# Groups of small products in seven forms among the warm-up products of a planned one-core kernel

## The chip, the cores and the metric

The kernel runs on one core of a Trainium2 chip. The metric is the device time of one execution in microseconds (us). The engines of a core work through queues of their own, in order: TensorE (PE, matrix products into PSUM; PEld is its weight load), VectorE (DVE), ScalarE (ACT), GpSimd (POOL), and SyncE (SP), which issues the DMAs.

## What is computed

The input x has 8 sequences of 512 rows and 128 columns, in fp32. Four blocks follow each other, each with a layernorm ahead and a residual: a scan (a gated state space model, "mamba"), a mixture of eight experts, a windowed attention with 16 heads, and the same mixture of experts again.

```
x = x + scan(layernorm(x))
x = x + experts(layernorm(x))
x = x + attention(layernorm(x))
x = x + experts(layernorm(x))

scan:      h = x W_in; xb, zb = halves of h, each: convolution over 3 steps, silu
           delta = softplus(dt W_dt + b_dt), clipped; b, c = tanh(...)
           decay = exp(-delta a), clipped;  state = decay * state + (1 - decay) * b * xb
           y = sum(state * c) + D * xb;     out = [y, zb] W_out
experts:   cw = softmax(x w_router) * softmax(10 x w_gating), normalised over the 8 experts
           out = sum over e of cw[e] * (silu(x w_gate[e]) * (x w_up[e])) w_down[e]
attention: softmax(q k + mask) v, chunks of 10 rows with 25 rows of left context
```

## The kernel before

Fp32 accuracy of the large products is reached with pairs: each operand is split into a rounded part and the rest (fp32r "hi" and "lo"), and one product becomes three (`matmul3`). An expert's work on one sequence is cut into four quarters of its 512 inner columns. A quarter has three products g (gate), three u (up) and three y (down). Between them ACT, DVE and POOL make h: silu of g, times u, the hi part, the lo part. For the first sequence the first four experts work on half a sequence (256 rows) at a time, the rest on 512.

The order of the instructions is written by a planner while the program is built. Each piece of work is a generator (a "lane") that yields the engine it needs next; `Clock` keeps an estimated end for every engine, and `Lanes.tick` (line 314) takes the lane that can start soonest. The estimated times only set the order: on the chip each engine runs its queue in order and waits on semaphores. All instructions pass through the wrapper `Engine`, so nearly every line of the profile names line 254 (`f(*args, **kw)`); groups are told apart by tile names.

Names that matter here. `x_m`, `tp_m`, `mxt`, `mh`, `mv`, `mxb`, `mzb`, `mde`, `mbc`: the scan block up to its rows. `mbx`: b spread over the state, then times xb; `mdec`: the decays, clipped on DVE by `cap`; `mst`: the scans; `mcc`, `mcx`: c times state; `macc`: their sum; `mo`: the output product. `tp_f`, `xt_f`, `lps`, `rps`, `pr`, `cw`, `cps`: layernorm, routing and weights of the experts; `cwb` is the weight of one expert spread over the partitions by a DMA, `y` times `cwb` is added up in `acc`, and `yp` transposes it back. `as`, `aw`, `ao`, `amt`: attention products in bf16 or with 32-column outputs. `wg`, `wu`, `wd` are the expert weights, loaded and split during the first 100 us.

The scan of the first sequence runs alone at the start, in two halves (`first_halves`, line 668), since the experts can't begin without it. The scan of sequence 1 runs beside the experts of sequence 0, and so on. ACT loads a function table whenever the next function isn't in the loaded one (line 533 and, without a call of `table`, line 254); `hidden` (line 1158) uses tanh and two DVE instructions instead of silu while the table with exp and tanh is loaded and the planner's clock is before `clock.hold`.

While the planner waits for the first expert inputs, the loop at line 1619 ticks the lanes; when none can start, it issues one dummy product into the bank `warm`, of the constant `sel` with itself (128x128 times 128x256, fp32r), and moves the planner's TensorE clock on by 0.1. Nothing reads `warm`. PSUM has eight banks; up to `AT_FIRST` = 7 of them may be held by work other than experts until the experts begin (`sides`, line 399), `warm` among them.

## Time and profile before

| | us |
|---|---|
| median of 3 runs | 1391.99 |
| lowest and highest of them | 1391.98, 1397.03 |
| the profiled execution, its own time | 1392.73 |
| its span, first to last instruction | 1390.9 |
| TensorE busy | 1353.4 (97%) |
| VectorE, ScalarE, GpSimd busy | 1053.2, 963.0, 944.5 |
| mean granted TensorE clock | 0.988 of full |

The profiled execution is one execution with the hardware profiler on. Its span runs from the first to the last instruction, and its own time holds some work around that. Rows of the order of time give start, duration, engine, line, operation, output tile, input tiles and shape; "[idle before <- X]" is the time that the engine waited and what ended it. Products on TensorE overlap, so the distance from start to start tells what one costs, not its duration.

### The profile page before, as it was taken

What the parts mean: (1) busy time and instruction counts of PE and PEld (TensorE: products, weight loads), DVE (VectorE), ACT (ScalarE), POOL (GpSimd) and SP (SyncE); (2) the same over time, 40 slices, a digit from 0 to 9 for tenths busy, and PEclk for the clock granted to TensorE, in tenths of its full rate; (3) what the DMA queues carried; (4) which work ended last, traced back from release to release, by engine and by line L of the source; (5) the groups of instructions that cost most, each with busy time, mean ns of one, the idle gap of its engine ahead of it and who ended that gap; (6) DMA issues with size and microseconds to landing.
All of it is one profiled execution on the core that took longest, in us unless ns stands there. A gap on an engine that the chain in (4) does not pass through costs nothing. (4 is left out here: it accounts for less than half of the span.)

```text
span 1390.9 us, 25797 instructions
## 1 busy us (share of the span) xinstructions
PE 1353.4 (97%) x8410; PEld 1085.0 (78%) x8410; DVE 1053.2 (76%) x3090; ACT 963.0 (69%) x1671; POOL 944.5 (68%) x1057
## 2 busy tenths in 40 slices
PE   7779999999999999999999999999999999999998
PEld 6677777777778878788788787787887877787886
DVE  6787888888986457888888888888888888754443
ACT  6568768677765557667777677777777776765654
POOL 4667576576674777666767667676666676777776
PEclk9989999999999999999999999999999999999999
DMA  3221214233126223356545455455564545222211
GB/s 123 73 82 35 69 39 125 59 81 91 35 54 81 55 52 65 84 110 125 129 88 125 100 117 137 78 128 115 105 141 78 116 64 100 53 66 53 39 39 38
DMA packets 256631, 116.28 MB, mean 84 GB/s; under 512 B 107996, under 2 KB 252401, under 8 KB 256497
## 3 DMA queue, kind: packets, MB, share of 16 engines
q1 hardware_dynamic: 256497, 114.64, 38.1%
q8 instruction: 66, 1.08, 0.3%
q14 instruction: 68, 0.56, 0.1%
HBM read 82.22 MB, written 31.98 MB: 82 GB/s over the span
## 5 line engine op out<-in xcount | busy, mean ns | idle before, releaser
L254 POOL TENSOR_TENSOR h<-h,h 128x512 fp32r<-128x512 f32 (+1 forms) x510 | 642.1, 1267 | 278.6 <-ACT h L254 242.5
L254 PE MATMUL u<-xt_f,wu 128*128 128x512 f32 (+1 forms) x1584 | 458.7, 398 | 10.3 <-ACT h L254 4.5
L254 PE MATMUL g<-xt_f,wg 128*128 128x512 f32 (+1 forms) x1584 | 454.4, 395 | 4.1 <-DVE mst L254 3.3
L254 PE MATMUL y<-h,wd 128*128 128x512 f32 (+1 forms) x1584 | 450.5, 394 | 1.9 <-POOL h L254 1.9
L254 ACT CAST h<-h 128x512 fp32r<-128x512 f32 (+1 forms) x476 | 286.4, 605 | 224.6 <-DVE h L254 222.3
L254 DVE TENSOR_TENSOR h<-u,h 128x512 f32<-128x512 f32 (+1 forms) x438 | 292.5, 673 | 180.3 <-PE u L254 126.0
L254 ACT ACTIVATE h<-g 128x512 f32<-128x512 f32 (+1 forms) x528 | 305.1, 583 | 116.2 <-PE g L254 90.2
L254 PEld LDWEIGHTS y<-h,wd 128*128 128x128 f32 x1584 | 290.9, 190 | 70.8 <-POOL h L254 3.0
L254 PEld LDWEIGHTS g<-xt_f,wg 128*128 128x128 f32 x1584 | 288.6, 190 | 70.2 <-DVE mst L254 4.0
L254 PEld LDWEIGHTS u<-xt_f,wu 128*128 128x128 f32 x1584 | 284.7, 189 | 74.9 <-ACT h L254 8.0
L254 POOL TENSOR_TENSOR acc<-acc,cwb 128x512 f32<-128x512 f32 (+1 forms) x115 | 146.9, 1278 | 54.9 <-DVE cwb L254 28.3
L254 DVE CUSTOM_DVE_ANT_0 amasked<-as,maskt 100x125 f32<-100x125 f32 (+2 forms) x640 | 141.6, 278 | 11.4 <-PE as L254 10.9
L254 ACT ACT_TABLE_LOAD x102 | 130.9, 1283 | 16.3 <-PE g L254 14.9
L254 DVE TENSOR_TENSOR apt<-aw,maskk 125x400 f32<-125x400 f32 (+2 forms) x160 | 89.7, 574 | 12.5 <-PE aw L254 12.4
L254 DVE TENSOR_TENSOR cwb<-y,cwb 128x512 f32<-128x512 f32 (+1 forms) x115 | 77.3, 672 | 16.6 <-PE y L254 9.6
L254 ACT ACTIVATE apt<-apt 125x400 f32<-125x400 f32 (+2 forms) x160 | 80.8, 540 | 0.4
L254 DVE SCALAR_TENSOR_TENSOR h<-h,g 128x512 f32<-128x512 f32 (+1 forms) x90 | 58.4, 651 | 18.4 <-ACT h L254 18.2
L254 DVE SCALAR_TENSOR_TENSOR h<-u,h 128x512 f32<-128x512 f32 (+1 forms) x90 | 58.8, 655 | 3.8
L254 PEld LDWEIGHTS <-ks 68*125 68x125 bf16 (+2 forms) x640 | 47.2, 136 | 11.4 <-issue 2.1
L254 PEld LDWEIGHTS <-qs 65*100 65x100 bf16 (+2 forms) x640 | 45.4, 125 | 11.0 <-issue 0.5
L254 DVE DVE_READ_ACCUMULATOR2_ANT amx<- 100x1 f32 (+2 forms) x640 | 51.5, 80 | 0.0
L254 PE MATMUL aw<-qs,ks 68*125 68x100 bf16 (+2 forms) x640 | 49.2, 220 | 0.5 <-DMA qs<-amts 0.5
(195 smaller groups left out, 1241.6 us busy)
## 6 DMA issues: line engine op xcount, KB each, us to landing
cwb<-cwd_f SPq DMA_DIRECT2D x124, 256.0 KB
aqd<-apc SPq DMA_DIRECT2D x64, 192.0 KB
ks<-aqd SPq DMA_DIRECT2D x48, 125.0 KB
qs<-aqd SPq DMA_DIRECT2D x48, 100.0 KB
x_fo<-x SPq DMA_DIRECT2D x16, 256.0 KB
aqd<-apc SPq DMA_DIRECT2D x32, 128.0 KB
x_f<-x SPq DMA_DIRECT2D x15, 256.0 KB
aod<-aos SPq DMA_DIRECT2D x24, 100.0 KB
```

Of the source, the lines that this page charges most:

```text
L254: f(*args, **kw)
```

## The change

`small` is a bf16 copy of the identity, made by one POOL instruction, in a buffer of the pool that later holds `cwb`. A second dummy bank, `warm2`, is taken beside `warm`, and `AT_FIRST` goes from 7 to 8, so that other work may hold as many banks as before. The waiting loop is as it was, but after the planner's time 8.0, and at most fourteen times, a group of small products comes ahead of the dummy: seven forms, each twice in turn. The forms differ in type (bf16 `small` or fp32 `ident`), in the rows of the array (68, 51, 48, 64 or 55, from row 0 or from row 64), in the columns of the output (125, two places of 50, four places of 30 or 32, all 128), in the order in which rows and banks alternate, and in their number (16, 32 or 4). Each product moves the planner's TensorE clock by 0.06 beyond its estimated cost. Nothing reads what they write.

```diff
-AT_FIRST = 7
+AT_FIRST = 8
 WARM = 3.5
+FORMS = 8.0
...
         warm = now(side([P, L], "warm"))
+        warm2 = now(side([P, L], "warm2"))
+        banks = warm, warm2
+        small = fp.tile([P, L], F32, tag="cwb", name="small", bufs=2).bitcast(BF16)[:, :P]
+        pool.tensor_copy(small, ident)
+        tried = []
+
+        def rows(n, t, k, into, form):
+
+            for i in range(n):
+                r = 64 * t(i)
+                form(i, slice(r, r + k), into(i))
+            clock.end["T"] += n * 0.06
+            return clock.end["T"]
+
+        def plain(i, r, o):
+            pe.matmul(o[:125, :100], small[r, :125], small[r, :100], start=True, stop=True)
+
+        def squares(i, r, o):
+            c = i % 2 * 64
+            pe.matmul(o[c : c + 50, :75], small[r, c : c + 50], small[r, :75], start=True, stop=True)
+
+        def strips(i, r, o):
+            c = i % 4 * 32
+            pe.matmul(o[c : c + 30, :55], small[r, c : c + 30], small[r, :55], start=True, stop=True)
+
+        def wide(i, r, o):
+            pe.matmul(o[:, :P], ident[r], ident[r], start=True, stop=True)
+
+        def thin(i, r, o):
+            c = i % 4 * 32
+            pe.matmul(o[c : c + 32, :30], ident[r, c : c + 32], ident[r, :30], start=True, stop=True)
+
+        forms = [
+            lambda: rows(16, lambda i: 0, 68, lambda i: banks[i % 2], plain),
+            lambda: rows(16, lambda i: i % 2, 51, lambda i: banks[i % 2], plain),
+            lambda: rows(16, lambda i: i // 2 % 2, 51, lambda i: banks[i // 2 % 2], plain),
+            lambda: rows(16, lambda i: i // 2 % 2, 48, lambda i: banks[i // 2 % 2], squares),
+            lambda: rows(32, lambda i: i // 4 % 2, 48, lambda i: banks[i // 4 % 2], strips),
+            lambda: rows(4, lambda i: i % 2, 64, lambda i: banks[i % 2], wide),
+            lambda: rows(16, lambda i: i // 4 % 2, 55, lambda i: banks[i // 4 % 2], thin),
+        ]
         while (0, 0) not in ready or ready[0, 0][1] == 0:
             if lanes.tick():
                 continue
             if clock.now > WARM:
                 sel = mc["sel"]
+                if clock.now > FORMS and len(tried) < 2 * len(forms):
+
+                    tried.append(forms[len(tried) % len(forms)])
+                    e = tried[-1]()
                 e = pe.matmul(warm[:, :HALF], sel[:, 0], sel[:, : HALF // P], start=True, stop=True)
                 clock.end["T"] += 0.1
             else:
                 clock.now += 0.03
+        freed(e)
         freed(e)
```

## The prediction

> **What bounds the kernel now.** I read the page's busy times first, then one row per stage, then who TensorE waited for, then the order of time in the stage that the change touches.

> ```profile
> PE 1353.4 (97%) x8410; PEld 1085.0 (78%) x8410; DVE 1053.2 (76%) x3090; ACT 963.0 (69%) x1671; POOL 944.5 (68%) x1057
> ```

> TensorE is busy for 1353.4 of 1390.9 us. The stage rows (length, busy time and instructions of PE, PEld, DVE, ACT, POOL, then granted clock, DMA share, GB/s) say where the other 37.5 us lie.

> ```profile
> 0.00:50.00 50.00, 38.29 (x224) 32.24 (x225) 35.29 (x86) 26.65 (x59) 23.20 (x36) 0.86 0.33 102
> 50.00:100.00 50.00, 38.34 (x237) 32.63 (x236) 39.60 (x94) 33.79 (x79) 35.46 (x49) 0.86 0.29 83
> 110.00:150.00 40.00, 37.84 (x177) 29.09 (x176) 30.96 (x63) 31.90 (x55) 27.14 (x32) 0.96 0.17 40
> 150.00:507.00 357.00, 353.47 (x1655) 278.76 (x1654) 281.65 (x522) 248.75 (x415) 236.62 (x234) 1.00 0.31 69
> 507.00:1380.00 873.00, 871.40 (x6033) 700.04 (x6032) 657.24 (x2305) 613.70 (x1047) 610.07 (x695) 1.00 0.44 91
> ```

> 23.4 us of TensorE's idle time lie in the first 100 us, at a clock of 0.86 instead of 1.00; 2.2 us between 110 and 150, 3.5 us between 150 and 507, 1.6 us from there to 1380, 7.0 us in the tail. The first 100 us are set by other engines, all the rest by TensorE. Who it waited for up to 96 us:

> ```profile
> PE u L254 <- DVE mst L254: 4.3, 1, 4.3
> PE tp_f L254 <- DVE xn_f L254: 3.8, 4, 1.8
> PE mbc L254 <- ACT mxb L254: 3.1, 1, 3.1
> PE g L254 <- DVE mst L254: 2.7, 1, 2.7
> ```

> These are the serial first sequence (mbc, tp_f) and, at 74 to 90 us, VectorE's scans (mst) of the second sequence, behind which the experts' gates queue on VectorE.

> **The change, part by part.** In the built instruction order of the changed kernel only twelve of the fourteen groups appear: the loop ends first, so wide and thin are there once. They hold 212 products; 27 of the 108 old dummies stay, 81 go.

> *Price of the products.* TensorE's order of time (start, duration, operation):

> ```profile
> 607.51 0.89 PE L254 MATMUL ao<-apt,v 125*32 125x100 f32 x32
> 608.33 0.96 PE L254 MATMUL y<-h,wd 128*128 128x512 f32 x3
> 609.13 0.21 PE L254 MATMUL amt<-eye,mp 110*80 110x110 bf16 x1
> 609.16 0.95 PE L254 MATMUL g<-xt_f,wg 128*128 128x512 f32 x3
> 609.94 0.62 PE L254 MATMUL aw<-qs,ks 68*127 68x102 bf16 x8
> 610.38 0.95 PE L254 MATMUL u<-xt_f,wu 128*128 128x512 f32 x3
> ```

> From start to start 8 aw take 0.44 us, 0.055 each; 32 ao take 0.82 us, 0.026 each. So 96 plain products cost 96 x 0.055 = 5.3 us and 32 squares 1.8. The 64 strips cost 1.7 at ao's row, 3.5 at aw's; I take 1.7, the row with the same 32-column outputs. For the fp32 ones the nearest rows are two mde of 64x256 at 65.28 to 65.92 us, 0.32 each, so half, 0.16, for 128 columns: 4 wide cost 0.6; and four lps of 128 columns at 66.97 to 67.53, 0.14 each: 16 thin cost 2.2 at most, 0.5 if their 30 columns count in proportion; I take 1.1. Together 10.5 us (9.7 to 13.4). A change of form costs about 0.09: the u after aw takes 0.79 to the next start (610.38 to 611.17), undisturbed ones 0.70. Twelve groups have 24 changes, 2.2 us. Removed are 81 x 0.126 (9 dummies from 7.74 to 8.88 us) = 10.2 us. All of this is at full clock; TensorE gets some 2.5 us more of filling, in windows where it would wait anyway. The copy of small is one POOL instruction (the cast of sel took 0.58 us for four times the columns) before sel, so the first dummies start 0.2 to 0.6 us later, with nothing behind them.

> [...]

> *Where a group is on the path.* Between mde and mbx the old order has 5 dummies and mbx starts at 16.49, 0.05 us after its operand. Now 16 squares and one dummy stand there: 0.9 + 0.13 from 15.39 us end at 16.4; at half clock at 17.4. Delay 0 to 0.9, taken as 0.3, since the clock row falls only in the stretch 16 to 18. The strips, wide and thin before mbx_1_0 (about 4 us with their changes, 8 at half clock, from 20.7 on) end by 29 us; VectorE wants that tile after its scan of 0_1, whose end was 28.9. The other groups stand before products that wait for VectorE anyway.

> ```profile
> 14.00:16.00 2.00, 1.83 (x9) 1.20 (x9) 0.54 (x2) 1.73 (x6) 1.74 (x2) 1.00 0.69 198
> 16.00:18.00 2.00, 1.76 (x9) 1.40 (x7) 1.09 (x3) 1.31 (x3) 0.59 (x2) 0.55 0.00 0
> ```

> The clock fell here after an idle stretch of 3.10 us. [...]

> *The planner.* Every dummy moves the planner's clock, so all later choices move. I compared the built orders of all five engines. From u of sequence 5, expert 3, last quarter, to the end they are equal, instruction by instruction: 5304 TensorE products, and with them POOL, ACT, DVE and SP. That product runs at about 507 us in the profile. The real products before it are the same set. So the last 884 us cost what they did: 0. Whatever the change gains or loses must lie in the first 507 us, where TensorE's whole idle time is 29 us.

> *Start, to 51 us.* VectorE's order now puts the multiplication of mbx_1_1 (0.67) and two more clips (0.35 each) before the residual of the first half, so its layernorm is about 1.1 us late, and both scans of the second half (0.68 + 0.68 + 1.37 us more) before the split of xt_f. The split ends near 42.0 us instead of 40.1; the first g comes near 44.5 instead of 40.72, since the output products of the first scan go before it. But the old order then lost 0.97 us at a u, 0.37 and 0.88 more, and had the second scan still to do. Followed on, both reach the end of y of the first block (three products each of g, u and y: 4 x 0.36 us) at 51 us, the new one by 0.5 us sooner. Taken as 0, bounds -1 to +3.

> *The second sequence, 51 to 99 us.* ACT:

> ```profile
> 70.79 0.39 ACT L254 ACTIVATE h<-g 128x256 f32<-128x256 f32 x1
> 71.19 1.28 ACT L533 ACT_TABLE_LOAD   x1
> ...
> 76.81 1.28 ACT L254 ACT_TABLE_LOAD   x1
> 78.11 0.94 ACT L254 ACTIVATE h<-g 128x256 f32<-128x256 f32 x3
> ```

> Two loads here; the new order has five (and two fewer later: 36 instead of 35 up to 507 us). Three more are 3 x 1.28 = 3.84 us on ACT, and queued behind them are mdec, the clips, the scans and the gates h. VectorE's instructions from the split of xt_f to mdelta sum to 25.2 us by their rows; with 4 to 6 us idle (9 of 30 before) mdelta ends at 71 to 73 us instead of 70.4, the first clip stands at 78 to 80 instead of 74.73. From first clip to the last macc it was 18.7 us (74.73 to 93.39) and is the same work: the end moves from 93.4 to about 98.5, +5.1 us. Against that five more expert blocks have passed VectorE by then, since the new order sets two or three gates between the scans: 5 x 3 x 0.36 = 5.4 us. Net -0.3, bounds -10 and +8 by the rivals. *99 to 507 us:* the stalls there were 5.7 us in all; another order of the same work gets others, 0 (bounds -4 to +4).

> *Sum.* 0.3 + 0 - 0.3 + 0 + 0 = 0 on the profiled execution (1392.7 us, span 1390.9, 1.8 around it), which is 0.7 above the median of the runs shown. I say **1393**, own range 1388 to 1399.

> **Rivals.** *The loads are not covered (slower).* If TensorE stands still for the three loads on ACT, its 4.3 us wait before the scans becomes 8.1, and the clock, which was half from 77.8 to 85.7 us and from 88 to 95, is half for one more stretch: 7 us of work at half rate lose 3.5. 3.84 + 3.5 = 7.3, so **1400**, more if a later sequence repeats it. It decides if the last macc ends after 93.4 + 5.4 = 98.8 us without more blocks done. For it: VectorE and ACT are in-order and 79% and 68% busy in 50 to 100. Against: the five blocks. *The interleaving pays (faster).* The 2.4 us around tp_f at 59 to 62, 4 of the 7.9 us idle between 73.8 and 89.8, and 3.5 us of half clock go: -9.9, **1383**. Against: VectorE was 4.96 of 5 us busy there. *The small forms do not hold the clock.* From 24 to 44 us some 3.7 us of real products run at half rate: +3.7, **1396**. *The change does not do what it says* is partly so: twelve groups, at no cost.

> **How the numbers follow.** Even 0.57, loads 0.21, interleaving 0.13, clock 0.09. 0.5% is 7 us, about what a measurement of this kernel can tell from no change: bounds 1385 and 1399. Faster 0.13, slower 0.21, within 0.66. The range 1386 to 1401 leaves about 0.1 on each side.

> **What would show it.** Right: the profile after 510 us equal row for row and shifted by a constant; twelve groups of some 0.9 us; five table loads between 70 and 90 us; the last macc of the second sequence at 97 to 100 us. Wrong: plain products over 0.1 us each at full clock, a TensorE idle sum in 0 to 507 us away from 29 by more than 5, or a different rate after 507 us.

## The result and the profile after

The kernel after takes 1401.16 us (median of 18 runs) against 1393.97 us of the kernel before, measured beside it (median of 18): ratio 1.0049, 95% interval 1.0035 to 1.0062, or 6.8 us more. A second measurement, beside later experiments, gave the same 1.0049 (1.0033 to 1.0065). The forecast was 1393 beside the 1391.99 us of the table of before, with the larger chance on "within 0.5%". In that measure the ratio makes 1398.8 us: just inside the 0.5% and the upper end of the own range, 1399, and nearer to the slower rival, 1400, than to the forecast.

The page's line of busy times of the kernel after (its profiled execution took 1400.3 us, span 1398.4, mean granted clock 0.981 instead of 0.988):

```profile
PE 1358.5 (97%) x8561; PEld 1086.9 (78%) x8561; DVE 1053.7 (75%) x3095; ACT 964.5 (69%) x1671; POOL 948.1 (68%) x1057
```

TensorE is idle for 39.9 us instead of 37.5 and busy for 5.1 us more, though its real products are the same. So most of the loss is work done more slowly. The stage rows of the kernel after (length, busy time of the five engines, granted clock, DMA share, GB/s), cut 7.5 us later from 507 us on:

```profile
0.00:50.00 50.00, 39.05 (x363) 31.11 (x364) 30.50 (x74) 26.39 (x58) 22.79 (x35) 0.73 0.33 102
50.00:100.00 50.00, 36.83 (x227) 31.56 (x227) 37.02 (x99) 38.32 (x79) 31.35 (x45) 0.86 0.25 69
110.00:150.00 40.00, 39.98 (x220) 32.27 (x220) 28.98 (x68) 32.85 (x61) 28.55 (x37) 1.00 0.16 44
150.00:514.50 364.50, 359.04 (x1675) 281.96 (x1674) 290.53 (x534) 248.64 (x418) 243.83 (x238) 1.00 0.31 68
514.50:1387.50 873.00, 871.72 (x6035) 700.52 (x6034) 657.42 (x2307) 614.07 (x1047) 612.06 (x696) 1.00 0.45 92
```

The last row is that of before (871.40 busy in 873 us) within 0.4 us: nothing was lost there. The first row has the clock at 0.73 instead of 0.86. Half clock lay at 16.2 to 23.0, 36.7 to 43.5, 77.6 to 84.5 and 87.9 to 94.7 us before, 27 us up to 110 us; after, at 14.2 to 31.3, 38.1 to 48.4, 58.6 to 62.0, 68.8 to 72.2, 85.9 to 92.7 and 103.0 to 109.8, 48 us.

Where the time was lost is seen by lining up equal work: TensorE's 8302 real products have a record in both traces, each is counted with its undisturbed interval at full clock, and the start of the same amount of work is compared. The table gives the kernel after minus the kernel before, at the time that the kernel before had reached, and the same for the experiments below:

| us later than before, at | 52 us | 81 us | 97 us | 102 us | 170 us | 486 us | ratio of times, 95% interval |
|---|---|---|---|---|---|---|---|
| after | +0.4 | -1.6 | +2.7 | +8.3 | +7.4 | +8.2 | 1.0049 (1.0035, 1.0062) |
| after, measured again | -0.3 | -3.9 | +1.0 | +5.1 | +4.3 | +5.1 | 1.0049 (1.0033, 1.0065) |
| e1 its order, no groups | -1.0 | -4.5 | +0.5 | +3.1 | +2.2 | +3.1 | 1.0027 (1.0017, 1.0038) |
| e2 its order, full dummies | +0.2 | -1.8 | +2.5 | +8.0 | +7.2 | +8.0 | 1.0036 (1.0021, 1.0051) |
| e3 old order, groups | +6.2 | +7.5 | +7.9 | +7.9 | +7.9 | +7.9 | 1.0049 (1.0032, 1.0066) |
| e4 after, three loads less | +0.3 | -1.8 | -0.4 | +2.3 | +1.5 | +2.3 | 1.0010 (0.9999, 1.0021) |
| e5 old order, no filling | +1.0 | +2.0 | +1.9 | +1.9 | +1.9 | +1.9 | 0.9996 (0.9986, 1.0006) |
| e6 before, three loads more | +1.6 | +7.8 | +6.5 | +6.5 | +6.5 | +6.5 | 1.0034 (1.0020, 1.0049) |
| e7 third order, no groups | -0.8 | -6.7 | -5.7 | -1.1 | +4.5 | +4.0 | 0.9995 (0.9983, 1.0007) |
| e9 its order, no groups, three loads less | -1.7 | -5.2 | -3.7 | -1.1 | -2.0 | -1.1 | 0.9999 (0.9985, 1.0012) |
| e10 third order, groups | +2.2 | -3.7 | -2.8 | +1.2 | +5.6 | +5.1 | 0.9999 (0.9987, 1.0011) |

One profile scatters by up to 3 us against another of the same kernel (the first two lines), and the profile of before is among its faster executions (1392.73 us against medians of 1394 to 1395), so entries are read as places and the ratios as sizes. In the kernel after, the loss is made between the 81 and the 102 us of before, at the end of the second sequence: from 1.6 us ahead to 8.3 behind. At 52 us it was even. The last 5.6 us of it are not peculiar to this kernel: from 97 to 102 us, where the second sequence of before is already done, e1, e4, e7 and e9 lose 2.6 to 4.7 us as well. In this profile these 5.6 us are 2.1 us of waiting and a stretch of half clock, 103.0 to 109.8 us. Rows of what TensorE waited for up to 112 us (us in total, times, longest):

```profile
PE y L255 <- DVE mst L255: 4.2, 1, 4.2
PE tp_f L255 <- DVE mst L255: 3.9, 1, 3.9
PE g L255 <- ACT h L255: 2.2, 1, 2.2
```

The scans (mst) of the second sequence still are the longest wait, 4.2 us (the 3.9 us of tp_f lie in the first sequence, up to 39.71 us), and a wait for a gate on ACT (h) has come in. ACT in that stretch, in order of time:

```profile
78.26 1.28 ACT L255 ACT_TABLE_LOAD   x1
79.55 0.23 ACT L255 ACTIVATE pr_f<-pr_f 128x32 f32<-128x32 f32 x1
79.80 1.28 ACT L534 ACT_TABLE_LOAD   x1
81.09 1.29 ACT L255 ACTIVATE mdelta<-mdelta 128x512 f32<-128x512 f32 x2
82.41 1.28 ACT L255 ACT_TABLE_LOAD   x1
83.70 0.38 ACT L255 ACTIVATE h<-g 128x256 f32<-128x256 f32 x1
84.10 1.28 ACT L534 ACT_TABLE_LOAD   x1
85.40 1.95 ACT L255 ACTIVATE mdec<-mdelta,nega 128x512 f32<-128x512 f32 x3
```

One small exponential of the router (pr_f) and one gate (h) stand between the second sequence's activations, and each makes the next instruction load its table anew: four loads here and a fifth at 88.12. Three rows of VectorE, the bounding of mdelta, the first clip and the last accumulation, first of the kernel before, then of the kernel after:

```profile
69.54 0.88 DVE L254 TENSOR_SCALAR mdelta<-mde,pa 128x256 f32<-128x256 f32 x2
74.73 0.73 DVE L254 TENSOR_SCALAR mdec<-mdec,cap 128x512 f32<-128x512 f32 x1 [0.47 <-ACT mdec L254]
92.70 0.69 DVE L254 TENSOR_TENSOR macc<-mcc,macc 128x512 f32<-128x512 f32 x1
```

```profile
78.41 0.88 DVE L255 TENSOR_SCALAR mdelta<-mde,pa 128x256 f32<-128x256 f32 x2
86.15 1.10 DVE L255 TENSOR_SCALAR mdec<-mdec,cap 128x512 f32<-128x512 f32 x2 [0.22 <-ACT mdec L255]
106.98 0.69 DVE L255 TENSOR_TENSOR macc<-mcc,macc 128x512 f32<-128x512 f32 x1
```

From the bounding of mdelta to the first clip it took 7.74 us; before, 5.19. The last macc ends at 107.67 us instead of 93.39, with five more expert blocks done.

### The profile page after: what moved, and what is told of

Read it like the earlier page. It is cut to its first block, busy times and chain, and to the rows that moved or that the text cites. A ratio compares the mean times of both kernels' runs of the same rounds, so it can differ in the third digit from the quotient of the medians.

```text
span 1398.4 us, 26106 instructions
## 1 busy us (share of the span) xinstructions
PE 1358.5 (97%) x8561; PEld 1086.9 (78%) x8561; DVE 1053.7 (75%) x3095; ACT 964.5 (69%) x1671; POOL 948.1 (68%) x1057
## 5 line engine op out<-in xcount | busy, mean ns | idle before, releaser
L255 ACT CAST h<-h 128x512 fp32r<-128x512 f32 (+1 forms) x469 | 282.0, 606 | 219.0 <-DVE h L255 216.7
L255 DVE CUSTOM_DVE_ANT_0 amasked<-as,maskt 100x125 f32<-100x125 f32 (+2 forms) x640 | 141.7, 278 | 11.2 <-PE as L255 10.6
L255 ACT ACT_TABLE_LOAD x102 | 130.9, 1283 | 16.2 <-PE g L255 14.7
```

## The experiments

Two causes were open: the new ORDER of all engines that the moved planner gives, and the small PRODUCTS themselves. The first three kernels part them. In these diffs `ghost` charges the planner's clock and issues nothing.

**e1: the order alone.**

```diff
 def plain(i, r, o):
-    pe.matmul(o[:125, :100], small[r, :125], small[r, :100], start=True, stop=True)
+    ghost.matmul(o[:125, :100], small[r, :125], small[r, :100], start=True, stop=True)
```

and so for the other four functions.

> The kernel after without its twelve groups of small products: the planner's clock is charged for them as before, so every other instruction of all five engines stands in the order of the kernel after. Theory ORDER (the loss comes from the second sequence's new order, which ends its scans late): as the kernel after, 1398 to 1403 us, ratio to before 1.003 to 1.007, and the last macc of the second sequence near 107 us (105 to 110). Theory PRODUCTS (the loss comes from the small products on TensorE and from the clock that they do not hold up): 1391 to 1395 us, ratio 0.998 to 1.001. With no filling, TensorE idles more before 45 us; by ORDER that costs at most 1 us, since VectorE leads there.

Measured: 1398.3 us against 1394.78, ratio 1.0027 (1.0017 to 1.0038), last macc at 104.1 us. The order alone is slower, by 3.7 us, which PRODUCTS excludes; it is also a little less than the whole, and the ratio and the last macc both fall just below what ORDER had expected. The rest, 3.1 us, would be the share of the products; the intervals of the two ratios just touch (1.0038 against 1.0035, and 1.0033 in the second measurement), so this share is likely and not more.

**e2: the order, with full dummies in place of the groups.**

```diff
                     e = tried[-1]()
+                    for _ in range(8):
+                        pe.real.matmul(warm[:, :HALF], sel[:, 0], sel[:, : HALF // P], start=True, stop=True)
```

on top of e1 (the dummies are the fp32r products of the kernel before).

> As the first kernel, but where a group stood, eight of the old 128x256 bf16 dummies are issued (8 x 0.126 = 1.0 us at full clock, about the length of a group). Theory ORDER: 1398 to 1403 us, ratio 1.003 to 1.007, last macc of the second sequence near 107 us. Theory PRODUCTS: near before, 1391 to 1396 us, ratio 0.998 to 1.002. If it is true that small products do not hold the clock, the granted clock, which in the kernel after is half from 14.2 to 31.3 us, comes back to full by 25 us here.

Measured: 1399.8 us, ratio 1.0036 (1.0021 to 1.0051), last macc at 107.4 us, and the clock back to full at 24.3 us, not at 31.3. So small products do hold the clock worse here, as was said, and yet the time hardly differs from that with the groups: a price of the half clock between 24 and 31 us doesn't show. Eight full dummies also take longer than a group (1.0 us at full clock against 0.7 on average), so this run doesn't part the two; e5 below does. The intervals of e2, e1 and the kernel after overlap, so this run does not rank them.

**e3: the products alone, in the old order.**

```diff
+                engine = pe
+                if clock.now > 8.0 and spent[0] < 84:
+                    engine = ghost
+                    if spent[0] % 7 == 0:
+                        tried.append(forms[len(tried) % len(forms)])
+                        tried[-1]()
+                    spent[0] += 1
-                e = pe.matmul(warm[:, :HALF], sel[:, 0], sel[:, : HALF // P], start=True, stop=True)
+                e = engine.matmul(warm[:, :HALF], sel[:, 0], sel[:, : HALF // P], start=True, stop=True)
```

and the functions of the change, with `r = 0` and the two halves of the bank `warm` in place of two banks.

> The kernel before with its own order on all five engines: from the planner's 8 us on, 84 of its dummies are left out and twelve groups of the small products stand in place of every seventh (all on the lower rows and in one bank, since the second bank is not there), and POOL makes the copy they read. Theory ORDER: as before, 1391 to 1396 us, ratio 0.998 to 1.002. Theory PRODUCTS: 1397 to 1402 us, ratio 1.003 to 1.006. If small products do not hold the clock, it stays half for more than the two stretches of before (16.2 to 23.0 us); by ORDER that costs at most 1 us, since VectorE leads up to 45 us.

Measured: 1400.62 us, ratio 1.0049 (1.0032 to 1.0066). ORDER fails here: in the old order the groups cost 6.8 us by themselves. The table says where: 6.2 us are lost by 52 us. The mh products start at 10.63 us (8.88 before), the first mbx at 19.18 (16.49), the first mo from mcx at 31.76 (27.04): the groups stand in TensorE's queue ahead of them, and the clock is half from 10.6 to 34.5 us. These groups, all on the lower rows and in one bank, are longer than those of the change: a group of 16 plain products of 51 rows took 1.06 us, the alternating ones of the change 0.60.

**e5: no filling at all, in the old order.** Is it that the groups stand in the way, or that the clock is half?

```diff
-                e = pe.matmul(warm[:, :HALF], sel[:, 0], sel[:, : HALF // P], start=True, stop=True)
+                engine = pe
+                if clock.now > 8.0 and spent[0] < 84:
+                    engine = ghost
+                    spent[0] += 1
+                e = engine.matmul(warm[:, :HALF], sel[:, 0], sel[:, : HALF // P], start=True, stop=True)
```

> The kernel before in its own order, with 84 of its dummies left out from the planner's 8 us on and nothing in their place. The third kernel of these experiments (groups in their place) was 6 us late by 50 us. Theory OCCUPANCY (the groups stand on TensorE ahead of the real products of the first sequence, at half clock for twice as long): without them the products of the first sequence are not held up, and the time is that of before, 1393 to 1396 us, ratio 0.998 to 1.002, although the clock stays half longer. Theory CLOCK (the real products between 10 and 45 us run at half clock, because the small ones do not hold it): 1398 to 1402 us, ratio 1.003 to 1.006, as with the groups, since with no filling the clock falls as well.

Measured: 1394.79 us, ratio 0.9996 (0.9986 to 1.0006). OCCUPANCY holds. 84 of the 108 dummies can go at no cost; TensorE then ran at half speed up to 31 us (four tp_m took 1.25 us instead of 0.60, eight mo at 27.13 us 2.07 instead of 1.16), and yet it was only 1.0 us late at 52 us. What cost 6.8 us in e3 was to stand in front of real products.

**e4: three table loads less, in the order of the change.**

```diff
+        if (k, b, t0) == (0, 0, 2):
+            nc.scalar.preload_act_table_set("natural_log_exp_and_others")
         act.activation(pr, pr, AF.Exp)
...
-                s = act.activation(h, g, AF.Silu)
+                swapped = nm == "0_0_0_256_1"
+                if swapped:
+                    nc.scalar.activation(h, g, AF.Exp)
...
```

and the fifth and sixth of the explicit loads in `table` are not issued, since the table is there.

> The kernel after with its groups and its order, but three of the five table loads on ACT between 78 and 89 us are gone: the table for the second sequence is loaded ahead of the router's exponential, and one gate (expert 0 of the first sequence, second half, second quarter) takes the exponential in place of silu, so that part of the output is another. Theory LOADS (what is wrong with the order are the 3 x 1.28 us on ACT ahead of the decays): the last macc of the second sequence comes about 4 us earlier, near 103.5 us, and the time is 3.8 to 7 us below the kernel after: 1394 to 1397 us, ratio 0.999 to 1.002. Theory INTERLEAVING (the order is late for what VectorE has to do between the scans, and ACT would have been waited for anyway): less than 2 us below the kernel after, 1399 to 1402 us, ratio 1.003 to 1.006.

Measured: 1394.82 us, ratio 1.0010 (0.9999 to 1.0021), 5.4 us below the kernel after by the ratios; last macc at 103.3 us. LOADS had said 3.8 to 7 us and 103.5. ACT in this kernel:

```profile
78.08 1.28 ACT L1029 ACT_TABLE_LOAD   x1
79.38 0.23 ACT L255 ACTIVATE pr_f<-pr_f 128x32 f32<-128x32 f32 x1
79.51 1.28 ACT L255 ACTIVATE mdelta<-mdelta 128x512 f32<-128x512 f32 x2
80.70 0.36 ACT L1181 ACTIVATE h<-g 128x256 f32<-128x256 f32 x1
80.96 1.94 ACT L255 ACTIVATE mdec<-mdelta,nega 128x512 f32<-128x512 f32 x3
```

The decays start at 80.96 us instead of 85.40, with everything before them where it was.

**e6: three loads more, in the kernel before.**

```diff
+            if len(explicit) == 5:
+                for other in ("exp_and_others", "silu_and_others", "exp_and_others"):
+                    nc.scalar.preload_act_table_set(other)
             nc.scalar.preload_act_table_set(name)
```

> The kernel before, with three more table loads (3 x 1.28 = 3.84 us) on ACT ahead of the second sequence's own load at 71.19 us, and nothing else. Theory LOADS: they are not covered: first mdec about 3.8 us later, last macc near 97 us instead of 93.4, and 3 to 7 us in the end: 1397 to 1401 us, ratio 1.002 to 1.005. Theory COVERED: TensorE has blocks enough to go on with: 1393 to 1396 us, ratio 0.999 to 1.001.

Measured: 1400.3 us, ratio 1.0034 (1.0020 to 1.0049), 4.7 us; last macc at 100.9 us. The two lines of it that decide, ACT's order of time and what TensorE waited for:

```profile
75.40 3.86 ACT L538 ACT_TABLE_LOAD   x3
```

```profile
PE u L254 <- DVE mst L254: 8.2, 1, 8.2
```

The one wait that was 4.3 us before is now 8.2: three loads pass through ACT, VectorE and TensorE without a loss on the way. COVERED is out. The last macc was expected near 97 us; this profile is 4.2 us late before the first of the loads (75.40 us instead of 71.19, with a stretch of half clock from 62.5 to 69.3 us), so its line in the table shows more than the loads, and their price is the wait and the ratio.

**e7: a third order.**

```diff
-            clock.end["T"] += n * 0.06
+            clock.end["T"] += n * 0.03
```

on top of e1.

> A third order: the planner's clock is charged 0.03 instead of 0.06 for each small product, and the groups are not issued. ACT then has no run of five loads in the second sequence, but two ahead of its decays, as in before; 25 expert blocks stand ahead of the second sequence's last product of macc (24 in the order of the kernel after, 19 before). Theory LOADS: about as before, 1392 to 1396 us, ratio 0.998 to 1.002. Theory ANY NEW ORDER (each order but the old one loses some 3 us): 1397 to 1400 us, ratio 1.002 to 1.004.

Measured: 1394.67 us, ratio 0.9995 (0.9983 to 1.0007). ANY NEW ORDER is out. This order is 5.7 us ahead at 97 us and 4.5 behind at 170 us, so it has a bad stretch of its own in between, whose cause is open.

**e9: the order of the change, no groups, three loads less** (e1 and e4 together).

> The kernel after without the groups (the planner's clock is charged for them, as in the first experiment, which stood at ratio 1.0027) and with three of the five table loads gone, as in the fourth (one gate of expert 0 takes the exponential in place of silu, so that part of the output is another). Theory LOADS (the whole cost of the new order is these loads): the 3.7 us of the order alone fall by 3.8 or more, to no loss against before: ratio 0.996 to 1.000, 1389 to 1395 us, last macc of the second sequence before 100 us. Theory REST (the order costs something else as well): ratio 1.001 or more.

Measured: 1394.36 us, ratio 0.9999 (0.9985 to 1.0012). LOADS holds: without these three loads the new order costs nothing that can be measured. Its last macc ended at 99.9 us; "before 100" was just met. The table says where the loads count: e9 and e1 differ by 0.7 us at 81 us and by 4.2 at 97, e4 and the kernel after by 0.2 at 81 and by 6.0 at 102.

**e10: the third order, with its groups** (the 0.03 of e7 in the kernel after; all fourteen groups come).

> The third order (0.03 charged for a small product), which without groups stood at ratio 0.9995, now with its groups issued, all fourteen of them. Theory PLACE (what the groups cost depends on where the order puts them ahead of the first sequence's products: about 3 us in the order of the kernel after, 6 to 7 in the order of before): between 1.001 and 1.005, 1396 to 1402 us, and the loss is there by 50 us. Theory ORDER ONLY (groups cost nothing but in the unlucky order): 0.998 to 1.001.

Measured: 1395.09 us, ratio 0.9999 (0.9987 to 1.0011). PLACE said 1.001 to 1.005 and missed, and of what it said only half is seen: TensorE is 3.0 us later than in e7 at 52 us, but 1.1 us at 486 us, and the times are the same. What the groups take from the first sequence is given back further on; that TensorE waits for VectorE there anyway would explain it, and is not shown.

**e11: the kernel after once more**, beside e9 and e10.

> The kernel after once more, beside the two others on one chip: 1.0035 to 1.0062 as before.

Measured: 1399.65 us, ratio 1.0049 (1.0033 to 1.0065).

**e8: each form by itself.** A stretch ahead of the first dummy repeats each form, with 96 full dummies before each; nothing else uses TensorE in it.

```diff
+            for n, t, k, f in (
+                (256, one, 68, plain), (384, lambda i: i % 2, 51, plain), (448, lambda i: i // 2 % 2, 48, squares),
+                (1024, both, 48, strips), (96, lambda i: i % 2, 64, wide), (1024, both, 55, thin),
+            ):
...
```

> Not a contest of times: the kernel after with a stretch put ahead of its first dummy, in which each form is repeated alone (256 plain of 68 rows, 384 plain of 51 rows on alternating halves, 448 squares, 1024 strips, 96 wide, 1024 thin), each after 96 full dummies. TensorE has no holes in it. Theory FORMS (small products do not hold the clock, however densely they come): the granted clock falls to half within some 7 us of the start of a form, in all of the small bf16 forms at least, and comes back within some 10 us of the next dummies. Theory HOLES (only waits let it fall): full all through, once it has risen.

The stage rows of this kernel, one for each form in that order (length, then PE's busy time and products, PEld's, the others, clock):

```profile
16.63:31.53 14.90, 14.90 (x258) 14.90 (x257) 0.00 (x0) 0.00 (x0) 0.00 (x0) 1.00 0.01 2
43.22:54.40 11.18, 11.18 (x385) 11.18 (x384) 0.00 (x0) 0.00 (x0) 0.00 (x0) 1.00 0.02 4
66.24:77.73 11.49, 6.31 (x448) 5.88 (x448) 0.00 (x0) 0.00 (x0) 0.00 (x0) 0.65 0.02 4
91.93:118.06 26.13, 9.75 (x1024) 8.89 (x1024) 0.00 (x0) 0.00 (x0) 0.00 (x0) 0.60 0.02 4
131.04:141.75 10.71, 10.71 (x192) 10.71 (x192) 0.00 (x0) 0.00 (x0) 0.00 (x0) 1.00 0.01 3
153.66:209.37 55.71, 23.78 (x2048) 22.05 (x2048) 0.00 (x0) 0.00 (x0) 0.00 (x0) 0.54 0.02 4
```

Neither theory holds as it was put. Both plain forms and the wide one keep full clock (1.00); squares, strips and thin lose it, 3.4, 5.0 and 4.7 us after their start, and dummies bring it back 5.4, 2.6 and 3.4 us after theirs (half clock at 69.6 to 83.2, 96.9 to 120.8 and 158.3 to 212.9 us). The busy column parts them: the three that hold keep TensorE busy all the time, the three that don't keep it busy for 55%, 37% and 43%, since in their long rows one pass comes every 0.0255 to 0.0272 us, alike in all three (an fp32 product is two: 2048 records for the 1024 thin ones). So a form does not lose the clock by the rows it fills: thin with 55 loses it and plain with 51 holds it. Two explanations stay: the idle time that these three leave on TensorE, and their narrow outputs (30 to 50 columns, against 125 and 128). No form here was narrow and kept TensorE busy, so the two are not parted.

## Why the prediction came out as it did

*The change's parts and their prices.* Twelve groups came, as said. Their sum, from the first start of each group to the next product, was 8.3 us, not 12.7 with the changes of form: the price 0.055 for the plain ones of 68 rows was right at full clock (0.058 in e8; 0.09 to 0.10 in the kernel after, at 30.04 us, where the clock was half up to 31.3, and at 5.94 us, where the dummies ahead came every 0.21 us instead of 0.126), and so was that of the wide ones (four took 0.65 us at full clock in e10, 1.16 at half clock here). The other forms were cheaper than their nearest rows: 16 alternating plain products took 0.60 us (0.0375 each), 32 strips 0.32 and 16 thin ones 0.39, both at half clock (0.85 and 1.1 were taken). A change of form, an estimate of 0.09 us in the prediction, cannot have cost much here: the twelve changes behind the groups are inside these 8.3 us, and the first group starts 0.21 us after the start of the last dummy ahead of it, the distance of the dummies themselves. Two figures of the working are off without consequence: the least of its price terms add up to 9.9 us, not 9.7, and the half clock of before ended at 84.5 us, not 85.7.

*Start, to 51 us: 0, bounds -1 to +3.* Right: the first y ran from 51.37 to 51.73 us where its end was put at 51, and equal work was 0.4 us late. Two parts that were not in the sum seem to cancel in it: against e1 the groups cost 1.4 us here (+0.4 against -1.0), and the order gave 1.0 back. These are single profiles, and the two of the kernel after differ by 0.7 us at this place. The rival "small forms do not hold the clock" named a true thing with a false price: the clock was half to 31.3 us, but the 3.7 us it asked for were not lost, for e5 ran at half speed for longer, from 6.6 us (four tp_m took 1.25 us instead of 0.60) to 31, and lost nothing (ratio 0.9996).

*The second sequence: net -0.3.* This step failed, and in the main the rival on the loads is what happened. Three terms of it were wrong. First, mdelta on VectorE was to end at 71 to 73 us, by 25.2 us of work and 4 to 6 us of waiting. The work was right (24.4 us busy from 42 to 79.1), the waiting was 12.7 us: VectorE waited for TensorE and for the gates on ACT, because TensorE, busy for 32.7 of these 37.1 us at a clock of 0.82, had more expert blocks in its queue ahead of mde (74.29 us instead of 65.28). An order was costed by one engine's sum where another engine's queue was in front. Some of this is the scatter of one profile: in e11 mdelta ends at 77.1 us, in e1 at 76.5, still 3.5 us or more later than was put. Second, the stretch from the first clip to the last macc took 21.5 us, not the 18.7 of before. Third, the loads: they were seen and counted (3.84 us), but set off against the five blocks as if both were the same time. The blocks were done, 24 instead of 19 at the last macc, and the loads were lost all the same: e4 gives back 5.4 us for three, e9 3.9 us on the order alone, and e6 loses 4.7 us for three in the old order. They stand in the one chain mdelta, mdec, clip, scan, and e6 shows them arriving at its end, in the wait for mst. In the kernel after gates (h) stand behind the same loads, and the waits are for mst (4.2 us) and for h (2.2 us), so there the share of the chain is argued, the cost of the loads shown. The rival's own arithmetic (a 4.3 us wait that becomes 8.1, and one more stretch of half clock) is what e6 measured for the wait (8.2).

The rival's point of decision, the last macc after 98.8 us "without more blocks done", did not decide: the macc came 8.9 us later than that, but five more blocks were done, and e4 (103.3 us), e7 (100.4), e9 (99.9) and e10 (102.5) pass it too without a loss. The end of the scans alone doesn't price an order. Of the prediction's signs, the last macc at 97 to 100 us failed, but none of those of being wrong came: up to 514.5 us TensorE is idle for 31.7 us, within 5 of 29, since most of the loss is work done more slowly.

*99 to 507 us: 0, bounds -4 to +4.* Right in sum: +8.3 us at 102 us of before, +8.2 at 486. In between 4.9 us were won (to 154 us of before) and lost again.

*After 507 us: 0.* Right: the row `as<-ks,qs` at 508.94 us stands at 516.48, 7.54 later, and the span ends 7.5 us later.

*The sum of the loss.* By the ratios, the loads explain 3.9 us (e1 to e9) to 5.4 us (after to e4) of the 6.8. The groups themselves would explain 3.1 us (e1 to after) with the loads and 1.5 us (e9 to e4) without. The first pair's intervals just touch and the second pair's overlap, so a cost of the groups in an order without the loads is not shown, and in the third order (e7, e10) none was measured. That the time came within 0.5% of before although this step failed is luck: the loads were counted rightly and set off against blocks that did not pay for them, and the whole loss, 6.8 us, happens to stay under the 7 us that 0.5% are. That "even" had 0.57 and "loads" 0.21 was the wrong way round.

## What to carry to other kernels

Where a planner's order is moved, list each serial chain's instructions on the engine that switches state (here table loads on ACT, 1.28 us each) and cost a switch inside the chain at its full length, however much other work is ready: finished blocks of another queue did not pay for it here (five of them, and e4 still gave back 5.4 us for three loads). Filling for the clock belongs where the next real product in TensorE's queue is not yet ready; in front of ready ones it held them up (6.2 us by 52 us in e3), and in the stage that other engines bound it may be worth nothing (84 of 108 dummies in e5). A third order with all fourteen groups at ratio 0.9999 shows that the change could be had for nothing; which order comes is decided by a few hundredths of a microsecond in the planner's prices.

## What the hardware showed that was not expected

The clock fell without one long wait too: the step before the fall at 36.7 us of before has two waits, of 0.85 and 0.90 us. In the traces of before and after it fell behind steps of this grid in which TensorE was busy for 1.67, 1.73, 1.76, 1.91, 1.99 and 2.04 of 3.41 us, and it held behind others with 1.69, 1.92 and 1.98, so that the recorded busy time alone gives no sharp border. Nor did one busy step always bring it back: in the kernel after TensorE is recorded as busy all through 17.64 to 24.46 us, two steps, and the clock stayed half to 31.3.

In a short burst the small products were far cheaper than in a row: in a group at half clock, 32 strips follow each other at 0.005 us (from 21.08 to 21.24 us in the kernel after, and 0.010 each with the time to the next product), where 1024 of them took 0.0255 us each in e8.
